# A conditioned feed-forward kernel with its opening rebuilt: who applies bias, deviation and shift, and in which order loads, VectorE's work and row stores stand

## The chip, the cores and the metric

The kernel runs on one core of one Trainium2 chip. A core has TensorE (matmuls, PE in the profile), VectorE (DVE), ScalarE (ACT), GpSimd (POOL) and SyncE (SP, which here only issues DMAs). ScalarE and GpSimd issue DMAs too. The metric is device time in microseconds: the median over runs of the whole execution.

## What is computed

`x` is 32 sequences of 128 tokens by 512 features, `cond` a row of 512 for each sequence, and `mask` marks tokens. With `m` the mask:

```python
emb = silu(t) @ ada_w + ada_b                       # (32, 1536)
shift, scale, gate_msa = split(emb, 3)
norm = layernorm(x) * (1 + scale) + shift
norm = where(m, norm, 0)
fwd = gelu(norm @ ssm_w1 + ssm_b1) @ ssm_w2 + ssm_b2
bwd = gelu(norm @ bwd_w1 + bwd_b1) @ bwd_w2 + bwd_b2
x = x + gate_msa * where(m, fwd + bwd, 0)
...
ff_norm = layernorm(x) * (1 + scale_mlp) + shift_mlp
h = gelu_tanh(ff_norm @ ff_w1 + ff_b1)
return x + gate_mlp * (h @ ff_w2 + ff_b2)
```

All is float32. The flips of the second branch cancel, as each token is worked on alone. The first half matters only for marked tokens, which are the last 0 to 32 of each sequence; the second half is for all 4096.

## The kernel before

The marked tokens are packed into 512 **slots**, four tiles of 128 (`NC`), in the order of their sequences. A matrix `pick` of 128 partitions by 512 slots says which sequence a slot belongs to; its 32 rows stand four times, once for each block of 128 features (`j`). Counting the slots of each sequence gives a column of token numbers, by which GpSimd gathers the tile's rows from `x` (`gather`, L277). Should there be more than 512 marked tokens, a loop at the end deals with the rest; it does nothing in these runs.

The first half works on the slots in two pairs of tiles. For tiles 0 and 1, in the opening:

1. `ada_w`'s shift and scale columns (`ada_a`, four blocks of 128 rows, L150) are loaded first. TensorE multiplies silu(cond), transposed (`sT`), by them into `pm_ss` (L633 to L635). The 32 rows of the four feature blocks lie in the four quarters of the partitions, so four matmuls share the array. The bias gets into the same bank by a matmul of its own, of `quarter` and the four rows `modb` (L294, L576). VectorE copies the sum out into `mod1` (L320).
2. TensorE spreads shift and scale over the slots, by `pick` (`of_slots`, L331; banks `part_s0`).
3. VectorE takes the statistics of a gathered tile (L159 to L162), GpSimd the root of the variance (L164). Then VectorE makes `(x - mean) * scale` in four strips (L356) and `* rstd + shift` in four more (L360).
4. TensorE transposes the tile (L194), ScalarE copies it out (L197), and TensorE multiplies by `w1`: `hidden_of_tile` for the first four blocks of the hidden layer, a tile at a time (L681), then `hidden` for the other four and both tiles together (L205). `w1` holds `ssm_w1` and `bwd_w1` side by side, `w2` both second matrices.

The slots' projections (`project`, L222) are finished by `finish_slots` (L378): gate, add `x`, statistics, and a store of the row with its mean and 1/deviation to `x1_wide` in DRAM. GpSimd gathers from there, over the loaded `x` tiles of the first eight sequences (`raw`, four tiles of two sequences), the rows that the first half changed (`take_first_rows`, L817). VectorE normalises these eight (L847): four are turned by VectorE and DMAs, four by TensorE (L950). All later sequences read `x1_rows`. The second half then runs over four pairs of four sequences each, as block products with sums in the manner of Strassen: `fw1_of.combine` (L403) and `weight_sums` (L741) make the sums of the weights. TensorE's matmuls L1123 and L1310 are this half.

The order on each engine is that of the source, since a manual schedule covers all five (L445). The names `on_zeros` and `keep_clock` are matmuls whose results nothing reads. Loads stand on SP's queue in the source's order; `load_behind_gathers` (L137) lets a GpSimd write to the tile first, so that the load is issued after the gather ahead of it on GpSimd. Each DMA of SP or ScalarE takes the next of eight semaphores, and its issue waits for the DMA that had it before.

Of the kernel before, what the change touches and what calls it, by code (L numbers as in the profile page):

```python
# [9 lines left out]
F32 = mybir.dt.float32  # L10
# [12 lines left out]
def kernel(  # L23
# [88 lines left out]
    nc.sync.dma_start(t_sb, cond)  # L112
# [37 lines left out]
    load_ada(ada_a, ada_w, range(KC), 2 * D)  # L150
# [143 lines left out]
    def modulation_bias(pm):  # L294
        nc.tensor.matmul(
            pm[:, : 2 * P],
            quarter,
            modb[:KC, :2],
            start=True,
            stop=True,  # L300
            skip_group_check=True,
        )

    def modulation_matmuls(pm, ada, lo, hi, blocks, begun=False):
        kinds = ada.rearrange("p k (m d) -> p k m d", d=D)
        for k in blocks:
            for j in range(KC):
                nc.tensor.matmul(
                    pm[ts(j, B), : (hi - lo) * P],
                    sT[:, k, :],  # L310
                    kinds[:, k, lo:hi, ts(j, P)],
                    start=(k == 0 and not begun),
                    stop=True,
                    skip_group_check=True,
                )

    def modulation_rows(pm, mod, lo, hi, bias=None):
        view = pm[:, : (hi - lo) * P].rearrange("p (m c) -> p m c", c=P)
        if bias is None:
            nc.vector.tensor_copy(mod[:, lo:hi], view)  # L320
            return
# [56 lines left out]
    def finish_slots(at, po, gate):  # L378
# [5 lines left out]
        nc.sync.dma_start(x1_wide[ts(at, P), :], t[:, 0])  # L384
        return lambda: nc.sync.dma_start(x1_rows[ts(at, P), :], row)
# [71 lines left out]
    nc.vector.memset(zeros, 0.0)  # L457
    pm_keep_clock = ps_h.tile([P, 512], F32, tag="h", name="pm_keep_clock")
# [73 lines left out]
    nc.gpsimd.tensor_scalar(modb[:KC, 1], modb[:KC, 1], 1.0, None, ALU.add)  # L532
# [43 lines left out]
    quarter = adap.tile([KC, P], F32, name="quarter")  # L576
    nc.scalar.copy(
        quarter.rearrange("p (j b) -> p j b", b=B), ident[:KC, :KC].unsqueeze(2).to_broadcast([KC, KC, B])
    )
# [34 lines left out]
    pick_slots(ts(1, NH))  # L614

# [3 lines left out]
    nc.vector.tensor_scalar(slot_of, slot_of, FAR, None, ALU.add)  # L619

# [16 lines left out]
    modulation_rows(pm, mod1, 0, 2)  # L637

    strips = of_slots(pick, (0, 1), mod1, slice(0, 2), 3 * [(ps_o, "o")] + [(ps_h, "h")], "part_s0")
# [3 lines left out]
    xn = group_of_tiles("s")  # L643
    xn_s = []
    for c in range(2):
        mv, rstd = statistics(xc[c : c + 1], f"s{c}")
        xn_s.append(
            modulated_by_strips(xc[c], strips, c, xn[:, c], mv[:, 0, 0:1], rstd, xn[:, 2 + c])
        )
        if c == 0:  # L650
            for n in range(2):
                nc.tensor.matmul(
                    pm_keep_clock[:, ts(n, 2 * P)], ident, xn[:, 2, ts(n, 2 * P)], start=True, stop=True
                )
            token_i = counted(slots_of_late, slot_col[:, NC // 2 :], NC // 2, "s1", ssm)
            late_slots()
            gather(xc[2], token_i[:, 0:1])
# [32 lines left out]
    transposed_slots(xn_s[0], xT_s[:, :, ts(0, P)], "s0")  # L690
    ptr = ps_t.tile([P, 512], F32, tag="tr", name="ptr_b")
    nc.tensor.transpose(ptr[:, :n_bias], bias_rows, ident[:n_bias, :n_bias])
    nc.tensor.transpose(ptr[:, n_bias : n_bias + B], slot_of, ident[:B, :B])
    nc.scalar.copy(biasT, ptr[:, :n_bias])
    slot_i = const.tile([P, B], I32, name="slot_i")
    nc.vector.tensor_copy(slot_i, ptr[:, n_bias : n_bias + B])
    for f in range(KC):
        hidden_of_tile(f, 0)
    transposed_slots(xn_s[1], xT_s[:, :, ts(1, P)], "s1")
# [90 lines left out]
    for c in range(2):  # L790
        if c == 0:
            own_statistics(raw[0], 2, "x_0")
# [37 lines left out]
    store_rows.append(finish_slots(1, project(1, h1, w2, "s1", seeded=po_s[1]), gs[1]))  # L830
    for i in range(2, 2 * G):
        take_first_rows(i)
# [26 lines left out]
    modulation_rows(pm, mod2, 0, 3, modb)  # L859
    normalised_of_side_0(range(2))  # L860
# [839 lines left out]
```

## Time and profile before

| What | Value |
|---|---|
| median of 3 runs | 452.73 us (452.65 to 452.76) |
| the profiled execution, own time | 453.43 us |
| its span | 451.7 us |
| TensorE busy | 444.0 us |
| VectorE busy | 334.5 us |
| ScalarE busy | 177.9 us |
| GpSimd busy | 158.4 us |
| HBM read, written | 56.71 MB, 13.70 MB |

The span runs from the first to the last instruction that the profiler saw; the execution's own time has some start and end around it. Busy shares are over the whole span, while the change is in its first sixth. For the opening one reads the timeline (start, length, engine, line, what is written from what, how many, and the idle time before them with what ended it). Each float32 matmul stands there as two rows. The DMA rows of the span's first stretch (us, moved until then, summed over all queues):

| until | 4 | 8 | 10 | 12 | 16 | 21.72 | 36.36 | 48.1 |
|---|---|---|---|---|---|---|---|---|
| MB | 0.39 | 2.06 | 2.43 | 3.11 | 4.53 | 6.67 | 12.48 | 16.76 |

Loads and their landing, as far as the trace shows them: the first gather is issued at 6.95 and lands after 3.7 us, the second 8.49 and 6.4; the third column block of `ada_a` 9.59 and 9.1; `ada_f`, the second half's conditioning matrix, has its last block issued at 33.3 and landed after 14.8.

### The profile page before, as it was taken

The page shows a single profiled execution, that of the slowest core. Times are in us where ns is not written, and L with a number is a line of the kernel's source. Part 1 is how long each engine was busy: PE and PEld are TensorE (multiplying, and loading weights), DVE is VectorE, ACT ScalarE, POOL GpSimd, SP SyncE. Part 2 cuts the span into 40 slices and gives each one's busy share as a digit, 9 for nine tenths or more (in the row PEclk, how much of TensorE's full clock was granted, in tenths as well). Part 3 has the DMA queues.
Part 4 walks back from the last instruction along what each step waited for, and adds up shares of the span by engine and source line. Part 5 has one row for each costly group of instructions (what it writes and reads, how often), then busy time and mean ns, then how long its engine had stood idle before and what let it go on. Part 6 is the DMA issues. An engine that isn't in the chain of part 4 may idle for free.

```text
span 451.7 us, 6204 instructions
## 1 busy us (share of the span) xinstructions
PE 444.0 (98%) x2147; PEld 370.2 (82%) x2147; DVE 334.5 (74%) x573; ACT 177.9 (39%) x389; POOL 158.4 (35%) x154
## 2 busy tenths in 40 slices
PE   8999999999999999999999999999999999999995
PEld 3884675688888888888888888888888888888884
DVE  5797788877799759977895689878956885434645
ACT  3123116353651551536526415464265244642000
POOL 4211470089770000897600007977000027560000
PEclk9999999999999999999999999999999999999999
DMA  6999449857327717741396177512971534122022
GB/s 250 372 399 408 177 65 308 284 187 229 129 97 168 108 49 268 235 138 36 105 177 93 46 267 230 141 38 86 189 99 47 176 128 129 35 93 95 0 94 96
DMA packets 85440, 70.84 MB, mean 157 GB/s; under 512 B 63396, under 2 KB 64508, under 8 KB 84382
## 3 DMA queue, kind: packets, MB, share of 16 engines
q1 hardware_dynamic: 64270, 57.76, 42.3%
q0 software_dynamic: 4160, 10.54, 6.9%
q10 hardware_dynamic: 16976, 2.11, 3.9%
q8 instruction: 18, 0.29, 0.3%
q14 instruction: 16, 0.13, 0.1%
HBM read 56.71 MB, written 13.70 MB: 156 GB/s over the span
## 4 chain that ended last, share of the span: by engine, by line
PE 84%; DMA 8%; DVE 3%; issue 2%; POOL 1%; SPq 0%; POOLq 0%
PE a_o L1310 24%; PE a_m L1123 21%; PE e_o L1310 18%; PE e_m L1123 16%; DMA fw<-in_L_cond_ff_w_dram 3%; PE po_s L222 3%; DMA w<-in_L_cond_bwd_w_dram 3%; DMA x_wide<-t_s 2%; DMA x<-x_wide,slot_i 1%; DVE t L403 1%; PE last L1310 1%; PE a_m_alone L1123 1%; POOL x L819 1%; PE ptr L950 0%; PE pl_s L255 0%
## 5 line engine op out<-in xcount | busy, mean ns | idle before, releaser
L1174 POOL TENSOR_TENSOR ha<-p_m,ha 128x512 f32<-128x512 f32 x20 | 25.8, 1292 | 176.0 <-ACT ha L1181 166.1
L1310 PE MATMUL e_o<-fw,ha 128*128 128x256 f32 x256 | 57.9, 379 | 0.0
L944 ACT ACTIVATE xT<-xT,modT 128x128 f32<-128x128 f32 x112 | 44.0, 480 | 28.1 <-DMA xT<-xn 28.1
L1310 PE MATMUL a_o<-t,hb 128*128 128x256 f32 x240 | 54.1, 379 | 0.0
L1310 PEld LDWEIGHTS e_o<-fw,ha 128*128 128x128 f32 x256 | 48.6, 190 | 6.6
L1310 PEld LDWEIGHTS a_o<-t,hb 128*128 128x128 f32 x240 | 45.6, 190 | 6.2
L1085 ACT ACTIVATE hb<-hb,biasT 128x256 f32<-128x256 f32 x64 | 29.0, 500 | 28.3 <-POOL hb L1207 16.1
L1137 ACT COPY p_m<-e_m 128x512 f32<-128x512 f32 x27 | 15.8, 586 | 51.6 <-PE e_m L1123 51.6
L890 POOL DMA_INDIRECT x<-x_rows,slot_i x24 | 27.2, 1135 | 6.2 <-issue 5.4
L1174 POOL TENSOR_TENSOR hb<-p_m,hb 128x512 f32<-128x512 f32 x20 | 29.2, 1460 | 0.3
L1310 PE MATMUL a_o<-fw,ha 128*128 128x256 f32 x128 | 28.9, 379 | 0.0
L1310 PE MATMUL a_o<-t,s 128*128 128x256 f32 x128 | 28.9, 379 | 0.0
L1310 PE MATMUL e_o<-fw,s 128*128 128x256 f32 x128 | 28.9, 379 | 0.0
L222 PE MATMUL po_s<-w,h_s 128*128 128x512 f32 x64 | 28.4, 594 | 0.0
L1181 ACT COPY ha<-e_m 128x512 f32<-128x512 f32 x32 | 18.5, 579 | 24.8 <-PE e_m L1123 24.4
L1310 PEld LDWEIGHTS a_o<-fw,ha 128*128 128x128 f32 x128 | 24.3, 190 | 3.3
L1310 PEld LDWEIGHTS a_o<-t,s 128*128 128x128 f32 x128 | 24.3, 190 | 3.3
L1310 PEld LDWEIGHTS e_o<-fw,s 128*128 128x128 f32 x128 | 24.3, 190 | 3.3
L1148 DVE TENSOR_TENSOR e_m<-a_m,ha 128x512 f32<-128x512 f32 x20 | 14.0, 698 | 17.0 <-POOL ha L1174 7.6
L1085 ACT ACTIVATE ha<-e_m,biasT 128x256 f32<-128x256 f32 x48 | 20.0, 468 | 14.4 <-PE e_m L1123 14.4
L1123 PE MATMUL a_m<-xT,tw 128*128 128x256 f32 x96 | 24.7, 380 | 0.0
L1123 PE MATMUL e_m<-s,fw 128*128 128x256 f32 x92 | 23.7, 380 | 0.0
(234 smaller groups left out, 894.1 us busy)
## 6 DMA issues: line engine op xcount, KB each, us to landing
x<-in_x_dram SPq DMA_DIRECT2D x16, 512.0 KB, 5.9
tw<-t_rows SPq DMA_DIRECT2D x16, 512.0 KB, 4.3
gate<-gate_rows POOLq DMA_DIRECT2D x8, 1024.0 KB, 5.1
out_dram<-x SPq DMA_DIRECT2D x15, 512.0 KB, 4.7
tw<-t_rows SPq DMA_DIRECT2D x16, 384.0 KB, 3.9
xT<-xn SPq DMA_DIRECT2D x80, 64.0 KB, 2.7
ada_f<-in_L_cond_ffada_w_dram SPq DMA_DIRECT2D x4, 768.0 KB, 14.8
ada_a<-in_L_cond_ada_w_dram SPq DMA_DIRECT2D x4, 512.0 KB, 3.6
```

The costliest lines, as they stand in the source:

```text
L222: nc.tensor.matmul(po, h[f][:, ts(i, P)], w[:, f, :], start=(f == 0 and seeded is None), stop=(f == HC - 1), skip_group_check=seeded is no ...
L403: engine.tensor_tensor(out, x, y, ALU.subtract)
L819: nc.gpsimd.indirect_dma_start(out=raw[i // 2][:, i % 2], out_offset=None, in_=x1_wide[:slots], in_offset=bass.IndirectOffsetOnAxis(ap=slo ...
L890: nc.gpsimd.indirect_dma_start(out=xs[i // G][i % G // 2][:, i % 2], out_offset=None, in_=x1_rows, in_offset=bass.IndirectOffsetOnAxis(ap= ...
L944: nc.scalar.activation(out, src, AF.Identity, bias=shift, scale=scale)
L1085: nc.scalar.activation(dst[:, n], src[:, n], AF.Gelu_apprx_tanh, bias=biasT[:, f : f + 1])
L1123: nc.tensor.matmul(bank[:, ts(n, QT)], self.w_block(j, product)[:, ts(n, P)], self.x_block(j, product), start=(product in ("P1", "P5") and ...
L1137: nc.scalar.copy(p5, e)
L1148: nc.vector.tensor_tensor(e, a, p5, add)
L1174: nc.gpsimd.tensor_tensor(self.place(RESULT[j], c), self.p5[j], other, ALU.add)
L1181: nc.scalar.copy(self.place(RESULT[j], c), src)
L1310: nc.tensor.matmul(part, src[:, k, ts(i, P)], w[product][:, k, :], start=(last and k == 0), stop=True, skip_group_check=True,)
```

## The change

- **Bias.** The bias matmul, `quarter` and GpSimd's addition of 1 are gone. `modb` is loaded as rows repeated for 32 sequences, and VectorE adds it as it takes scale and shift out of `pm_ss`, one after the other. The last block of `ada_a` is loaded and multiplied in two halves, scale first. `pm_ss` has a bank of `ps_h`.
- **Deviation and shift.** For tiles 0 and 1 VectorE makes only `(x - mean) * scale`. The transposes become matmuls: of the tile by a diagonal matrix `unit` with 1/deviation on it (ScalarE makes it from the identity), added to a matmul of `shift_of`, the shift in four diagonal blocks, by `pick`. Four plain matmuls and four transposes' worth of matmuls stand where four transposes stood. For tiles 2 and 3 nothing changes here.
- **Scale strips** are made for one tile at a time, the second tile's between the first tile's transposes and its hidden layer.
- **Loads.** `ada_a` is first on SP; `cond` goes to ScalarE's queue, behind the mask. The first four column blocks of `w1` come in two halves, each behind a gather, and the gate columns of `ada_a` after them, behind no gather of their own.
- **Order.** The transposes of the bias rows and of `slot_of` go ahead of the last block of `pm_ss`, and `slot_of` ahead of the late `pick`. The statistics of `raw[0]` go behind the two late tiles, those of `raw[2]` behind the second finish and the gathers of `raw[1]`, those of `raw[3]` behind `mod2`, with the gathers of each tile behind its statistics.
- **Row stores.** The first `x1_wide` store is issued by ScalarE.
- **Filler.** One `on_zeros(256)`, one round of `keep_clock` and the two matmuls on the scaled tile are gone.

The diff, cut to its core:

```diff
-    nc.sync.dma_start(t_sb, cond)
+    nc.scalar.dma_start(t_sb, cond)
...
-    nc.sync.dma_start(modb[:KC, :2], ada_b[: 2 * D].rearrange("(m j c) -> j m c", m=2, c=P))
...
-    load_ada(ada_a, ada_w, range(KC), 2 * D)
+    load_ada(ada_a, ada_w, range(KC - 1), 2 * D)
+    for m in (1, 0):
+        nc.sync.dma_start(ada_a[:, KC - 1, ts(m, D)], ada_w[ts(KC - 1, P), ts(m, D)])
+    for m in (1, 0):
+        load_conditioning_bias(modb[:, m : m + 1], ada_b, (m,))
...
-    nc.gpsimd.tensor_scalar(modb[:KC, 1], modb[:KC, 1], 1.0, None, ALU.add)
+    xn = group_of_tiles("s")
+    shift_of = xn[:, 2].rearrange("p (j c) -> p j c", c=P)
+    unit = [xn[:, 3, ts(c, P)] for c in range(2)]
+    nc.gpsimd.memset(shift_of, 0.0)
...
-        if c:
-            on_zeros(256)
...
-            load_behind_gathers(w1[:, :, :D], ssm_w1)
-    load_behind_gathers(ada_a[:, :, 2 * D :], ada_w[:, 2 * D :])
+            load_behind_gathers(w1[:, :, : D // 2], ssm_w1[:, : D // 2])
+    load_behind_gathers(w1[:, :, D // 2 : D], ssm_w1[:, D // 2 :])
+    load_blocks(ada_a[:, :, 2 * D :], ada_w[:, 2 * D :])
...
-    pm = ps_o.tile([P, 512], F32, tag="o", name="pm_ss")
-    modulation_bias(pm)
-    modulation_matmuls(pm, ada_a, 0, 2, range(KC), begun=True)
+    modulation_matmuls(pm_ss, ada_a, 0, 2, range(KC - 1))
+    ptr = ps_t.tile([P, 512], F32, tag="tr", name="ptr_b")
+    nc.tensor.transpose(ptr[:, :n_bias], bias_rows, ident[:n_bias, :n_bias])
+    nc.tensor.transpose(ptr[:, n_bias : n_bias + B], slot_of, ident[:B, :B])
...
+    for m in (1, 0):
+        modulation_matmuls(pm_ss, ada_a, m, m + 1, (KC - 1,), m)
+    nc.vector.scalar_tensor_tensor(mod1[:, 1], pm_ss[:, ts(1, P)], 1.0, modb[:, 1], ALU.add, ALU.add)
+    nc.vector.tensor_tensor(mod1[:, 0], pm_ss[:, ts(0, P)], modb[:, 0], ALU.add)
+
+    in_four = 3 * [(ps_o, "o")] + [(ps_t, "tr")]
+    scales = of_slots(pick, (0,), mod1, slice(1, 2), in_four, "scale_s0")
     slots_of_late = slots_to_count(pick[:, NH:], NC // 2, "s1", (ps_h, "h"))
...
-    keep_clock(2, 0)
...
+    for j in range(KC):
+        nc.scalar.copy(shift_of[ts(j, B), j], mod1[ts(j, B), 0])
+
+    def with_shifts(c, banks):
...
+        for k in range(KC):
+            nc.tensor.matmul(
+                parts[k],
+                shift_of[:, k],
+                pick[:, ts(c, P)],
+                start=(k % each == 0),
+                stop=False,
+                skip_group_check=True,
+            )
+        return t, parts
+
+    def scaled_slots(c, scales):
         mv, rstd = statistics(xc[c : c + 1], f"s{c}")
...
+        nc.scalar.activation(unit[c], ident, AF.Identity, scale=rstd[:, 0:1])
+        for j in range(KC):
+            nc.vector.scalar_tensor_tensor(
+                xn[:, c, ts(j, P)],
+                xc[c][:, ts(j, P)],
+                mv[:, 0, 0:1],
+                scales[j][:, 0, 0],
+                ALU.subtract,
+                ALU.mult,
+            )
+
+    def in_features(c, t, parts):
+        for k in range(KC):
+            nc.tensor.matmul(
+                parts[k], xn[:, c, ts(k, P)], unit[c], start=False, stop=True, skip_group_check=True
+            )
...
+    keep_clock(1, 0)
+    parts_0 = with_shifts(0, ((ps_t, "tr"), (ps_h, "h")))
+    scaled_slots(0, scales)
+    in_features(0, *parts_0)
+    scales = of_slots(pick, (1,), mod1, slice(1, 2), in_four, "scale_s1")
+    token_i = counted(slots_of_late, slot_col[:, NC // 2 :], NC // 2, "s1", ssm)
+    late_slots()
+    gather(xc[2], token_i[:, 0:1])
+    scaled_slots(1, scales)
...
-    transposed_slots(xn_s[0], xT_s[:, :, ts(0, P)], "s0")
...
     for f in range(KC):
         hidden_of_tile(f, 0)
-    transposed_slots(xn_s[1], xT_s[:, :, ts(1, P)], "s1")
+    in_features(1, *with_shifts(1, ((ps_t, "tr"),)))
...
-    own_statistics(raw[1], 2, "x_1")
+    for n in range(2):
+        own_statistics(raw[n], 2, f"x_{n}")
...
-    own_statistics(raw[2], 2, "x_2")
...
-    store_rows = [finish_slots(0, project(0, h1, w2, "s0", seeded=po_s[0]), gs[0])]
+    store_rows = [finish_slots(0, project(0, h1, w2, "s0", seeded=po_s[0]), gs[0], nc.scalar)]
...
-    own_statistics(raw[3], 2, "x_3")
...
-    for i in range(2, 2 * G):
+    store_rows.append(finish_slots(1, project(1, h1, w2, "s1", seeded=po_s[1]), gs[1], nc.sync))
+    for i in range(2, G):
+        take_first_rows(i)
+    own_statistics(raw[2], 2, "x_2")
+    for i in range(G, G + 2):
         take_first_rows(i)
...
     modulation_rows(pm, mod2, 0, 3, modb)
+    own_statistics(raw[3], 2, "x_3")
+    for i in range(G + 2, 2 * G):
+        take_first_rows(i)
```

More of the change, by code (lines that the diff above doesn't have):

```diff
@@ L292, in late_slots, with modulation_matmuls @@
         xc.extend(both[:, c] for c in range(NC // 2))
[L294 to L304, printed above, removed]
+    def modulation_matmuls(pm, ada, lo, hi, blocks, at=0):
         kinds = ada.rearrange("p k (m d) -> p k m d", d=D)
@@ L308, in modulation_matmuls @@
                 nc.tensor.matmul(
-                    pm[ts(j, B), : (hi - lo) * P],
+                    pm[ts(j, B), at * P : (at + hi - lo) * P],
                     sT[:, k, :],
                     kinds[:, k, lo:hi, ts(j, P)],
-                    start=(k == 0 and not begun),
+                    start=(k == 0),
                     stop=True,
@@ L315, in modulation_matmuls, with modulation_rows @@
                 )
-    def modulation_rows(pm, mod, lo, hi, bias=None):
+    def modulation_rows(pm, mod, lo, hi, bias):
         view = pm[:, : (hi - lo) * P].rearrange("p (m c) -> p m c", c=P)
-        if bias is None:
-            nc.vector.tensor_copy(mod[:, lo:hi], view)
-            return
         other = slice(0, hi - lo, 2)
@@ L376, in gates_of_slots, with finish_slots @@
         return [t[:, n] for n in range(len(tiles))], to_sbuf
-    def finish_slots(at, po, gate):
+    def finish_slots(at, po, gate, queue):
         t = tp.tile([P, 1, D + 2], F32, tag="t", name=f"t_s_{at}")
@@ L383, in finish_slots @@
         own_statistics(t, 1, f"s_{at}_x1")
-        nc.sync.dma_start(x1_wide[ts(at, P), :], t[:, 0])
+        queue.dma_start(x1_wide[ts(at, P), :], t[:, 0])
         return lambda: nc.sync.dma_start(x1_rows[ts(at, P), :], row)
@@ L457 @@
     nc.vector.memset(zeros, 0.0)
+    pm_ss = ps_h.tile([P, 512], F32, tag="h", name="pm_ss")
     pm_keep_clock = ps_h.tile([P, 512], F32, tag="h", name="pm_keep_clock")
@@ L575 @@
     nc.scalar.copy(sT.rearrange("p k b -> p (k b)"), ptr[:, : KC * B])
[L576 to L579, printed above, removed]
     warm = stp.tile([1, 1], F32, tag="warm", name="warm", bufs=1)
@@ L613 @@
     load_blocks(w2[:, :KC], ssm_w2)
-    pick_slots(ts(1, NH))
     slot_of = adap.tile([B, S], F32, name="slot_of")
@@ L619 @@
     nc.vector.tensor_scalar(slot_of, slot_of, FAR, None, ALU.add)
+    pick_slots(ts(1, NH))
     mod1 = const.tile([P, 3, P], F32, name="mod1")
@@ L631, in keep_clock @@
                 )
-    pm = ps_o.tile([P, 512], F32, tag="o", name="pm_ss")
-    modulation_bias(pm)
-    modulation_matmuls(pm, ada_a, 0, 2, range(KC), begun=True)
+    modulation_matmuls(pm_ss, ada_a, 0, 2, range(KC - 1))
+    ptr = ps_t.tile([P, 512], F32, tag="tr", name="ptr_b")
+    nc.tensor.transpose(ptr[:, :n_bias], bias_rows, ident[:n_bias, :n_bias])
+    nc.tensor.transpose(ptr[:, n_bias : n_bias + B], slot_of, ident[:B, :B])
+    nc.scalar.copy(biasT, ptr[:, :n_bias])
+    slot_i = const.tile([P, B], I32, name="slot_i")
@@ L636 @@
+    nc.vector.tensor_copy(slot_i, ptr[:, n_bias : n_bias + B])
+    for m in (1, 0):
[4 more added lines that the diff above has]
+    scales = of_slots(pick, (0,), mod1, slice(1, 2), in_four, "scale_s0")
     slots_of_late = slots_to_count(pick[:, NH:], NC // 2, "s1", (ps_h, "h"))
-    modulation_rows(pm, mod1, 0, 2)
@@ L639 @@
-    strips = of_slots(pick, (0, 1), mod1, slice(0, 2), 3 * [(ps_o, "o")] + [(ps_h, "h")], "part_s0")
-    keep_clock(2, 0)
     xT_s = ssm.tile([P, KC, NH], F32, tag="xT", name="xT_s0", bufs=2)
     xT_t = ssm.tile([P, KC, NH], F32, tag="xT", name="xT_s1", bufs=2)
-    xn = group_of_tiles("s")
-    xn_s = []
-    for c in range(2):
-        mv, rstd = statistics(xc[c : c + 1], f"s{c}")
[L647 to L657, printed above, removed]
+    for j in range(KC):
+        nc.scalar.copy(shift_of[ts(j, B), j], mod1[ts(j, B), 0])
@@ new lines, in with_shifts @@
+    def with_shifts(c, banks):
+        t = []
+        for pool, tag in banks:
+            t.append(pool.tile([P, 512], F32, tag=tag, name=f"ptr_s{c}_{len(t)}"))
+        each = KC // len(t)
+        parts = [t[k // each][:, ts(k % each, P)] for k in range(KC)]
+        for k in range(KC):
[8 more added lines that the diff above has]
+        return t, parts
@@ new lines, in scaled_slots @@
+    def scaled_slots(c, scales):
+        mv, rstd = statistics(xc[c : c + 1], f"s{c}")
+        nc.scalar.activation(unit[c], ident, AF.Identity, scale=rstd[:, 0:1])
[13 more added lines that the diff above has]
+            )
+        for half_no in range(2):
+            k = ts(half_no, KC // 2)
+            src = t[half_no % len(t)].rearrange("p (k s) -> p k s", s=P)
+            nc.scalar.copy(
+                xT_s[:, k, ts(c, P)], src[:, : KC // 2] if len(t) == 2 else src[:, k]
+            )
@@ L688, in hidden_of_tile @@
             )
-    transposed_slots(xn_s[0], xT_s[:, :, ts(0, P)], "s0")
[L691 to L696, printed above, removed]
     for f in range(KC):
         hidden_of_tile(f, 0)
-    transposed_slots(xn_s[1], xT_s[:, :, ts(1, P)], "s1")
+    in_features(1, *with_shifts(1, ((ps_t, "tr"),)))
     pm = ps_o.tile([P, 512], F32, tag="o", name="pm_g")
@@ L790 @@
     for c in range(2):
-        if c == 0:
-            own_statistics(raw[0], 2, "x_0")
         mv, rstd = statistics(xc[2 + c : 3 + c], f"s{2 + c}")
@@ L829 @@
         take_first_rows(i)
-    store_rows.append(finish_slots(1, project(1, h1, w2, "s1", seeded=po_s[1]), gs[1]))
-    for i in range(2, 2 * G):
+    store_rows.append(finish_slots(1, project(1, h1, w2, "s1", seeded=po_s[1]), gs[1], nc.sync))
[3 more added lines that the diff above has]
+    for i in range(G, G + 2):
         take_first_rows(i)
```

## The prediction

> **What bounds the kernel now.** I read the page's first part, then the chain of waits of the first 90 us, then the timeline, engine by engine. The page says what the end is made of:
>
> ```profile
> PE 444.0 (98%) x2147; PEld 370.2 (82%) x2147; DVE 334.5 (74%) x573; ACT 177.9 (39%) x389; POOL 158.4 (35%) x154
> ```
>
> TensorE (PE) works or is kept warm nearly always, so a gain is an earlier arrival of its useful work; nothing after the opening is touched. The chain (start, length, what) shows where its queue last waits for someone else:
>
> ```profile
> 10.01 11.69 DMA w<-in_L_cond_bwd_w_dram
> 21.72 14.63 DMA fw<-in_L_cond_ff_w_dram
> 36.37 1.24 DVE t L403
> ...
> 41.38 0.61 DVE st_x L172
> ...
> 46.39 4.75 DMA x_wide<-t_s
> ...
> 54.37 0.58 POOL t_s L176
> 54.97 2.96 DMA x_wide<-t_s
> ...
> 63.43 3.87 DMA x<-x_wide,slot_i
> 67.30 0.03 issue
> 67.32 0.56 DVE xn L847
> 67.92 0.33 PE ptr L950
> ```
>
> Up to 67.92 us the chain is not TensorE's: the load of `fw1`, VectorE's sums, the store of the first slots' rows, eight gathers by GpSimd, the eighth normalised tile. From there TensorE runs without a break that counts. What TensorE did meanwhile, and how near it came (start, length; in brackets the idle time and its releaser):
>
> ```profile
> 7.63 3.64 PE L308 MATMUL pm_ss<-ada_a,sT 128*32 128x256 f32 x32
> 13.08 1.07 PE L625 MATMUL pm_keep_clock<-ada_a,sT 128*32 128x256 f32 x16
> 16.24 3.81 PE L681 MATMUL ph_s<-xT_s,w 128*128 128x128 f32 x32 [0.27 <-issue]
> 19.88 0.60 PE L194 MATMUL ptr_s<-ident,xn_s 128*128 128x128 f32 x4
> 20.41 1.08 PE L308 MATMUL pm_g<-ada_a,sT 128*32 128x128 f32 x32
> 21.58 3.84 PE L681 MATMUL ph_s<-xT_s,w 128*128 128x128 f32 x32
> 66.31 0.49 PE L950 MATMUL ptr<-ident,xn 128*128 128x128 f32 x3
> 67.92 0.33 PE L950 MATMUL ptr<-ident,xn 128*128 128x128 f32 x1 [1.12 <-DVE xn L847]
> ```
>
> So **two paths meet at 67.92**: TensorE's own work, which could have gone on at 66.80 (67.92 - 1.12), and the side chain. The change shortens both. What it is worth is the later of the two.
>
> **TensorE's path, up to the first hidden matmul (L681, 16.24).** A recorded pair is one float32 matmul, so 32 rows are 16 matmuls.
>
> Removed ahead of `pm_ss`: `on_zeros(256)` between the two slot counts (L462, 5.74 to 6.06) and the bias matmul (L295, 6.65 to 7.63). The weights of `pm_ss` are not late: the DMA rows give 2.06 MB moved by 8.0 us, nearly all of `ada_a`, whose last block was used at 10.2. So `pm_ss` starts 1.3 us sooner, at about 6.3. Three of its four blocks take 3 x 0.854 = 2.56 us (3.64 us for four, less the tail), to 8.9; the two transposes of `ptr_b`, moved here, 0.3; the last block in two halves, 2 x 0.43, to 10.05. `modb` arrives as 64 KB broadcasts instead of 4 KB, on a DMA idle then (55 to 109 GB/s at 8.3 to 8.9 us); I cost it nothing, and 1:1 if it lands after 9.8.
>
> VectorE: the second token column was done at 7.69, now about 7.5; three `slot_of` operations (1.1), the late pick (0.85), `slot_i` (0.18), then scale and shift (0.29 each, the row of L323): mod1 is complete at about 10.4. It was 11.76 after the copy L320. But now the first gathered tile binds: issued at 6.95, landed after 3.7 us, at 10.65. The gather's issue needs nothing that moves. Its statistics: 0.69 + 0.18 + 0.15 with gaps, to 11.75; then only four strip operations instead of eight (1.12 for four): 12.9. GpSimd's root (0.58) and ScalarE's scaled identity (0.3, as the copy L577) end at 12.8 beside them. The four ScalarE copies of the shift (0.25 each, near L575's 0.27) end at 11.5.
>
> TensorE meanwhile: scale strips to 10.65, late count 0.86, `keep_clock(1, 0)` 0.85, to 12.3; four shift matmuls and four deviation matmuls, 0.228 each if the clock is full (3.81 us less tail, over 16): 13.2 and 14.1. ScalarE copies a half in 0.33, and the next scale strips take 0.2: **the first hidden matmul at 14.25** instead of 16.24. Its weights: the first half of `w1` needs some 0.4 MB after 3.11 MB at 12.0, the second follows by 14.5 and is used at 16.1.
>
> **The second tile gives much of it back.** Four transposes took 0.53 us (19.88 to 20.41); four shifts and four deviations are 8 x 0.228 = 1.83. From first to second hidden stretch were 5.34 us (21.58 - 16.24): hidden 3.75, transposes 0.53, `pm_g` and the count 1.06. It becomes 14.25 + 3.75 + 1.83 + 1.02 + 0.25 = 21.1. So **TensorE gains only 0.5 us**. VectorE is done with that tile at 16.2 and hides. The gate columns of `ada_a` landed at 18.7, with 0.13 MB more ahead of them 19.0; `pm_g` wants them at 19.8.
>
> Here a rule speaks against the change. The Trainium skill, "TensorE: Matmul & The Clock Gate", section "What's actually happening": a window of 3.4 us decides, and a busy one lifts the half clock. Row first: `pm_ss` took 634 ns a pass, the same form under `keep_clock` 379; the strips (L342) fall from 548 to 374 between 11.83 and 12.1. The clock rose at 12.0 though TensorE had been busy since 3.26[...]. The page's PEclk shows 9 throughout, so it doesn't show this. By the rule the denser stretch from 6.3 would lift the clock at the boundary before, 12.0 - 3.4 = 8.6: strips at 14.0, TensorE's gain 0.75. By the row it is 12.0 again; I take the row. Against: the change takes out filler (one `on_zeros`, four `keep_clock` matmuls, two on `xn`). If the window to 12.0 is not full enough, 15.4 is next.
>
> **The side chain.** The DMA stream decides up to `fw1`: 6.67 MB by 21.72, 12.48 MB by 36.36, about 396 GB/s. The same bytes stand ahead of `fw1`, and the stream starts at 9.6 in both, for the first `w1` load still waits for the first gather (issue 8.31). The SP queue's issue of `fw1` waits for the landing of `bwd_w1` as before. `fw1` lands at 36.3 again, give or take 0.5, and VectorE's sums end at 41.38. The bound is now: `own_statistics(raw[2])` (41.38 to 43.10, 1.7 us) no longer precedes `finish_slots(0)`, whose projection ends at 41. The store's issue moves from 46.39 to 44.65.
>
> Its landing took 4.75 us behind `ada_f` and the biases on SP's queue, the lighter one at 54.97 took 2.96. From ScalarE's queue: the skill, "DMA: Bandwidth & Descriptors", "Issuing engines are not separate DMA queues", says that all queues share 16 engines and another issuer only saves issue time. By that 4.75: lands 49.4; by the nearest row 2.96: 47.6. I take 48.5, for `ada_f` flows till 48.1 and the rings interleave. Behind this store on ScalarE wait the last seed (0.59) and the late copies at 49.1; ScalarE was idle 6.05 us there. GpSimd follows as before (first gather to last landing: 0.81 + 11.48 + 3.87 after the store lands), plus 0.65 for the root of `raw[3]`, now between gathers: 48.5 + 16.0 = 64.5, and the tile is normalised at 65.1.
>
> VectorE takes the moved statistics back: the second finish starts when TensorE's projection ends, 48.66 - 0.5 = 48.15, and lasts 2.55; statistics 1.7; mod2 0.65; statistics 1.75; two tiles 2.4; sums 2.05; two tiles 2.4; 0.3; sums 2.1; four tiles 2.0: **66.05**. It was 67.88. Its `turn` stores start 0.4 us sooner; ScalarE's scaling ended at 79.85 against a use at 82.7, so they stay hidden.
>
> **Sum.** TensorE could go on at 66.80 - 0.5 = 66.3; VectorE is done at 66.05, gathers at 65.1. The resumption moves from 67.92 to 66.3: **1.6 us**. The profiled execution took 453.43 (span 451.7, 1.7 around it), and becomes 451.8; the median of 452.73 is 0.70 below it, so I forecast **451.1**.
>
> **Rivals.**
> - *More*: the clock rises at 8.6, or the first tile lands sooner on the emptier DMA, and TensorE gains 1.4. Then VectorE's row above also starts 0.9 sooner, gathers end at 65.1, and the gain is 2.5: **450.2**. For it: only half of `w1` now stands ahead of the second gather, and TensorE has no gap from 6.3 on. Against: the first gather's 3.7 us, which nothing here shortens.
> - *Given back*: the first hidden matmul no sooner than 15.3 (late `t_sb` on ScalarE's queue behind the mask delays the counts beyond its 0.6 us slack, late `modb`, a gather later by 1 us). TensorE then loses 0.5; 1.12 - 0.5 = 0.6 us: **452.1**, no change to be told. For it: three things now arrive within half a microsecond of their use.
> - *Slower*: the clock stays half until 18.8, the second boundary after 12.0. Shifts and deviations cold take 3.4 instead of 1.83, the first hidden matmul comes at 16.0, and at half speed does 1.4 us of its work by 18.8; the second stretch starts at 24.2, 2.6 late. With 1.12 of slack that is 1.5: **454.2**. It decides once the loss exceeds 1.12. For it: the clock took until 12.0 with more filler. Against: the window from 8.6 is still filled by `pm_ss`, strips, counts and four keep-clock matmuls.
> - *It doesn't do what it says*: the ScalarE store lands no sooner. At 49.4 the last tile is ready at 66.0, still in time; no loss.
>
> **Numbers.** Forecast 0.42, more 0.30, given back 0.15, slower 0.13. A measurement here tells 0.2% (0.9 us) from nothing: faster than 451.8 holds the first two, 0.72; within 0.15; slower 0.13. The range goes from 449.8 (gain 2.9, the store landing at 47.6 and all else hidden) to 452.9 (the whole of the given-back case); the likeliest case alone is 450.7 to 451.6.
>
> **What would show it.** First hidden matmul near 14.25 and second near 21.1; `pm_ss` from 6.3; strips at the fast rate by 12; first row store issued near 44.7 and landed by 48.5; the last transposes of `raw[3]` near 66.3 with no wait to speak of. Wrong if `pm_ss` waits for `ada_a` or for ScalarE's `sT`, if hidden matmuls run cold, if `fw1` lands after 37.5, or if a wait beyond 70 us eats the shift.

## The result, and the profile after

The changed kernel took 457.73 us (median of 4 runs, 456.18 to 458.13) beside 452.75 us for the kernel before on the same chip: ratio 1.0101, interval 1.0075 to 1.0126, **slower by 5.0 us**. Run once more on another chip it took 456.53 (6 runs, 455.56 to 458.85) beside 452.98: 1.0082, interval 1.0061 to 1.0104. A ratio is estimated from the fast executions of both kernels, so it can differ a little from the quotient of the medians. The two profiled executions have spans of 456.4 and 454.9 us (own times 458.13 and 456.70) against 451.7 (453.43) before. Line numbers are those of each kernel's own profile; the changed file is some 30 lines longer from the opening on (L950 became L981, L222 became L225).

TensorE's total hardly moved; the time is in when its work comes. The page's first part:

```profile
PE 445.2 (98%) x2164; PEld 371.7 (81%) x2164; DVE 332.4 (73%) x566; ACT 180.0 (39%) x394; POOL 158.8 (35%) x154
```

The chain of waits of the first changed execution (start, length, what) shows both ends of the loss:

```profile
1.25 4.68 DMA t_sb<-in_cond_dram
5.93 0.02 issue
5.95 0.64 ACT s_sb L564
6.59 0.04 issue
6.63 0.63 PE ptr_s L568 x4
...
60.01 0.85 POOL x L179
...
64.02 0.73 POOL x L179
...
66.38 3.80 DMA x<-x_wide,slot_i
70.18 0.02 issue
70.21 0.56 DVE xn L875
70.77 0.04 issue
70.81 0.47 PE ptr L981
71.28 3.14 PE po_s L225 x4
74.43 0.44 PE ptr L981 x4
```

At the top, the load of the condition, now on ScalarE's queue, lands at 5.93; before, `s_sb` started at 2.72. Below, the eighth gather is issued at 66.38 (before 63.43), with two roots of GpSimd (`POOL x L179`) between the gathers, and TensorE resumes at 70.81 (before 67.92): 2.9 us. The next group (74.43) comes 4.45 us later than before: `po_s` took 3.14 us instead of 1.72. The third of the three parts is a wait of 0.36 us near 93.6 us. 2.9 + 1.4 + 0.4 = 4.7, the difference of the spans. Why `po_s` is slow shows in the windows of that stretch (window, its length, TensorE's busy time and records, granted clock, DMA share, GB/s):

```profile
68.00:70.00 2.00, 0.77 (x5) 1.00 0.94 113
70.00:71.00 1.00, 0.19 (x1) 0.81 1.18 199
71.00:72.00 1.00, 1.00 (x3) 0.50 1.33 113
72.00:73.00 1.00, 1.00 (x3) 0.50 1.43 146
73.00:74.00 1.00, 1.00 (x2) 0.50 1.06 193
74.00:76.00 2.00, 2.00 (x9) 0.99 1.01 393
```

TensorE was idle for most of 68 to 71, and the granted clock fell to half until 74. The second execution had as little work there (0.96 us in 68 to 71, as here) and kept a clock of 1.00. It lost 2.45 at the resumption (70.37) and 0.36 at the later wait, of 3.2 in all. So the resumption is what both share. Its timeline in that execution, TensorE first, then GpSimd (start, length, engine and line, operands, in brackets the idle time and its releaser):

```profile
15.98 3.93 PE L716 MATMUL ph_s<-xT_s,w 128*128 128x128 f32 x32
22.79 3.84 PE L716 MATMUL ph_s<-xT_s,w 128*128 128x128 f32 x32
67.52 0.38 PE L981 MATMUL ptr<-ident,xn 128*128 128x128 f32 x2
68.55 0.33 PE L981 MATMUL ptr<-ident,xn 128*128 128x128 f32 x1 [0.65 <-DVE xn L875]
70.37 0.33 PE L981 MATMUL ptr<-ident,xn 128*128 128x128 f32 x1 [1.49 <-DVE xn L875]
```

```profile
46.33 0.87 POOL L179 TENSOR_TENSOR t_s<-t_s,half 128x1 f32<-128x1 f32 x1 [8.38 <-issue]
53.47 1.09 POOL L844 DMA_INDIRECT x<-x_wide,slot_i  x1 [6.26 <-DMA x_wide<-t_s]
...
59.27 1.02 POOL L179 TENSOR_TENSOR x<-x,half 128x2 f32<-128x2 f32 x1
...
63.44 0.72 POOL L179 TENSOR_TENSOR x<-x,half 128x2 f32<-128x2 f32 x1
...
65.79 1.12 POOL L844 DMA_INDIRECT x<-x_wide,slot_i  x1 [0.31 <-issue]
```

TensorE could have gone on soon after 68.0; the side chain ends last, and it is late by parts that add up. Before, the root of the first finish began at 45.80 and took 0.56, the first gather came at 51.95, the eighth at 63.43. Now the root begins 0.53 later, takes 0.31 longer, the row store from its end to the first gather takes 6.27 instead of 5.59 (0.68), and from first gather to eighth are 12.32 us instead of 11.48 (0.84). Sum 2.36; the eighth was issued 2.36 later.

The first part, 0.53, hides more. The statistics that were moved away took 1.8 us ahead of this finish, and still it starts later, since all before it is late. The opening of this execution shows why (TensorE's two groups, GpSimd's first gather, VectorE's first use of `fw1`):

```profile
6.07 0.63 PE L568 MATMUL ptr_s<-ident,s_sb 32*128 32x32 f32 x4 [0.83 <-ACT s_sb L564]
6.51 1.20 PE L258 MATMUL pl_s<-rank,pick 32*128 32x128 f32 x4
8.42 1.18 POOL L281 DMA_INDIRECT xc<-in_x_dram,token_i_s  x1 [4.45 <-DVE before_s L264]
38.73 1.23 DVE L393 TENSOR_TENSOR t<-fw 128x1024 f32<-128x1024 f32 x1 [1.55 <-DMA fw<-in_L_cond_ff_w_dram]
```

The same gather before:

```profile
6.95 1.24 POOL L278 DMA_INDIRECT xc<-in_x_dram,token_i_s  x1 [2.85 <-DVE token_i_s L270]
```

The slot counts (`pl_s`, of which the gather's token numbers are made) stand behind `ptr_s` in TensorE's queue, and `ptr_s` waits for the condition. So the gather is issued 1.47 us later, the loads behind it start later, and `fw1` is used 2.36 later (before 36.37). The mask is late too, though it did not change its queue, as `ada_a` now goes ahead of all else. First execution, then before:

```profile
4.15 0.21 DVE L529 CAST mask_f<-mask_u 32x128 f32<-32x128 uint8 x1 [2.54 <-DMA mask_u<-in_mask_BxS_bk_dram]
```

```profile
2.88 0.23 DVE L535 CAST mask_f<-mask_u 32x128 f32<-32x128 uint8 x1 [1.28 <-DMA mask_u<-in_mask_BxS_bk_dram]
```

### The profile page after: what moved, and what is told of

Same layout as the page of the kernel before. It is cut to its first block, busy times and chain, and to the rows that moved or that the text cites. A ratio compares the mean times of both kernels' runs of the same rounds, so it can differ in the third digit from the quotient of the medians.

```text
span 456.4 us, 6244 instructions
## 1 busy us (share of the span) xinstructions
PE 445.2 (98%) x2164; PEld 371.7 (81%) x2164; DVE 332.4 (73%) x566; ACT 180.0 (39%) x394; POOL 158.8 (35%) x154
## 4 chain that ended last, share of the span: by engine, by line
PE 93%; DMA 2%; DVE 2%; POOL 2%; issue 1%; ACT 0%; ACTq 0%; POOLq 0%; DVEq 0%
PE a_o L1341 23%; PE a_m L1154 21%; PE e_o L1341 18%; PE e_m L1154 16%; PE po_s L225 6%; PE ph_s L716 2%; PE ph_s L208 2%; POOL x L844 1%; DMA t_sb<-in_cond_dram 1%; DMA x<-x_wide,slot_i 1%; PE pm_ss L301 1%; PE a_m_alone L1154 1%; PE last L1341 1%; PE ptr_s L649 0%; PE ptr_s L674 0%
## 5 line engine op out<-in xcount | busy, mean ns | idle before, releaser
L225 PE MATMUL po_s<-w,h_s 128*128 128x512 f32 x64 | 29.9, 619 | 0.0
```

Of the source, the lines that this page charges most:

```text
L225: nc.tensor.matmul(po, h[f][:, ts(i, P)], w[:, f, :], start=(f == 0 and seeded is None), stop=(f == HC - 1), skip_group_check=seeded is no ...
```

## The experiments

Three theories stood at the start: 1, the small loads moved behind `ada_a` hold the engines; 2, TensorE's own rebuilt work costs; 3, the new order of VectorE's work and the row store cost. The first four runs split the change. Medians beside the kernel before on the same chip; the ratio with its interval.

**The opening alone** (every hunk but the tail's order, gathers and row store).

> The rebuilt opening with all its loads, but with VectorE's order, the gathers and the row store as they were before. Theory 1: the opening holds the whole loss, so 457 to 459 us. Theory 3, the order and the row store: if statistics moved between finish, gathers and normalisation, and the store from ScalarE, are what is late, the time falls to 454 to 455.5.

456.7 us against 453.15: 1.0076 (1.0059 to 1.0093). **The tail's order alone:**

> The kernel before with VectorE's new order, the split gathers and the first row store from ScalarE alone. Theory 1: no loss here. The store issues near 44.7 instead of 46.39 and, at the 5.4 us that it took in the changed kernel, lands near 50.1 instead of 51.14; the last tile is ready near 66.6 instead of 67.88, and TensorE resumes at 66.8: 451.4 to 452.0 us. Theory 3: slower than 453.5.

454.23: 1.0026 (1.0018 to 1.0035). So both halves lose, 3.6 and 1.1 us, and together about what the whole does. The first theory was right on the first, 0.3 us below its range, and wrong on the second. In the opening's profile, its slowest execution (458.50), TensorE comes to the last transposes without a wait and is itself late; more on this under its clock:

```profile
71.39 0.60 PE L978 MATMUL ptr<-ident,xn 128*128 128x128 f32 x4
```

**Only cond on ScalarE's queue**, in the kernel before:

```diff
-    nc.sync.dma_start(t_sb, cond)
+    nc.scalar.dma_start(t_sb, cond)
```

> The kernel before with that one line alone: cond on ScalarE's queue behind the mask; SP starts with the 4 KB of bias and then ada_a, 0.4 us sooner than before. Theory 1: cond is used after 5 us instead of 2.72, TensorE's counts start near 6.3 instead of 5.04, the first gather near 8.2 instead of 6.95, and the time rises by 1 to 2 us (453.7 to 454.8), because everything behind the gather shifts. Theory 2: within 0.5 us of 452.7.

453.67: 1.0012 (1.0005 to 1.0019), 0.5 us: half of what the first theory had at the least, and the most that the second allowed. In its profile TensorE waited 1.38 us for `s_sb`, the first gather was issued 0.95 later, the second hidden stretch started 1.43 later, but the last transpose at L950 only 0.2 later: the old opening had 1.1 us of slack there. And **cond first on SP's queue again**, in the changed kernel, the same line the other way round:

> The changed kernel with one line put back: cond is loaded first on SP's queue again. Theory 1, the small loads: on ScalarE's queue mask and cond (4 and 64 KB) shared the 16 engines with 2 MB of ada_a that SP issued at 0.81, so mask was used at 4.15 instead of 2.88 and cond at 5.95 instead of 2.72; TensorE's counts wait behind cond's transposes, and gather, loads of w1 and fw1 behind the counts. Then mask is used by about 3.3, cond by 3.0, the first gather issues near 7.2 instead of 8.99, the first hidden matmul comes near 14.8 instead of 16.61, fw1 lands near 37.6 instead of 39.4, and the time falls by 2 to 3.5 us from 457.7, to 454.2 to 455.7. Theory 2, the matmuls: what costs is the rebuilt transposes and the new order; the time stays above 456.5 and TensorE still loses to the kernel before between first and second hidden stretch only.

458.46: 1.0127 (1.0105 to 1.0149), no better. The mask was used at 2.82 again, and `pm_ss` did start at 6.24, but the first hidden matmul came at 18.88, not near 14.8. The wait came back one step on, in TensorE's timeline of this kernel:

```profile
6.24 2.79 PE L301 MATMUL pm_ss<-ada_a,sT 128*32 128x256 f32 x24
11.18 0.25 PE L623 MATMUL ptr_b<-ident,bias_rows 16*128 16x16 f32 x1 [2.15 <-DMA bias_rows<-in_L_cond_ff_b_dram]
11.49 1.08 PE L301 MATMUL pm_ss<-ada_a,sT 128*32 128x128 f32 x16
```

The third of the small `bias_rows` loads was issued at 7.48 on ScalarE's queue and landed past 11. The change had set `ptr_b`, which needs it, ahead of the last block of `pm_ss`, which does not; in TensorE's queue the block waited with it. In the changed kernel the late condition had hidden this.

**Both holds removed** (cond first, and the six lines of `ptr_b` back ahead of the first hidden layer), once with the changed tail and once with the old:

> The changed kernel with cond first on SP's queue again and ptr_b's two transposes, biasT and slot_i back ahead of the first tile's hidden layer. Theory A (TensorE's in-order queue was held by small loads: 2.15 us for bias_rows at ptr_b, after 1.4 us for cond): no wait at ptr_b, first hidden matmul at most 16.9 us in place of 18.88, and at least 1.5 us less than the 458.46 of the kernel with cond alone moved: 456.0 to 457.0. Theory B (TensorE stays at half its clock, since the rebuilt opening gives it less to do): first hidden matmul comes forward by less than 1 us since the cold stretch is as long, time above 457.5. Theory C (the tail's order and ScalarE's row store set the end): 458.0 to 458.8, unchanged, since the side chain ends last.

> The same two repairs in the kernel with only the opening rebuilt (the tail's order, gathers and SP's row store as before). Theory A: with both holds gone the opening is no later than that of before; 452.5 to 454.0 against 453.1 of before. Theory B: 455.5 to 456.5 (456.7 without the repairs). Theory C: like A for this kernel, below 454, and the gap to the kernel with the changed tail is 2 us or more.

456.47 (1.0075, 1.0062 to 1.0088) and 455.01 (1.0047, 1.0030 to 1.0064) beside 452.86. Each taken against the kernel before on its own chip, the first loses 1.7 us less than with cond alone (3.6 for 5.3), the second 1.4 less than the opening with neither (2.15 for 3.55; the intervals just overlap). Against the changed kernel itself (1.0101, and 1.0082 when run again) the first gains 1 us or nothing. Its first hidden matmul stood at 18.73, where theory A had 16.9 at most, and TensorE came to L981 at 70.17 without a wait: its half rate lasted until near 18.8 there, as two rows of one form show.

```profile
14.20 2.08 PE L643 MATMUL ptr_s<-pick,xn_s 128*128 128x128 f32 x8
22.40 1.06 PE L643 MATMUL ptr_s<-pick,xn_s 128*128 128x128 f32 x8
```

So the holds are shown in the traces and in the opening's time; they are not all, and what they are worth in the changed kernel is not clear of noise. The second kernel's profile caught an early clock (about 10.5 us), and shows what the rebuilt opening is worth when all goes well:

```profile
15.14 3.84 PE L710 MATMUL ph_s<-xT_s,w 128*128 128x128 f32 x32
18.82 1.06 PE L643 MATMUL ptr_s<-pick,xn_s 128*128 128x128 f32 x8
19.71 1.06 PE L668 MATMUL ptr_s<-xn_s 128*128 128x128 f32 x8
20.70 1.08 PE L301 MATMUL pm_g<-ada_a,sT 128*32 128x128 f32 x32
21.86 3.84 PE L710 MATMUL ph_s<-xT_s,w 128*128 128x128 f32 x32
```

First hidden matmul 1.1 us sooner than before (16.24), second 0.3 later (21.58), since shifts and deviations of the second tile fill 18.82 to 20.70. In this execution the rebuilt arithmetic gives back more than it gains.

**TensorE's clock.** The first kernel has the opening rebuilt, both repairs, and the filler put back (`on_zeros(512, 512)` ahead of `pm_ss`, `on_zeros(256)` between the gathers, `keep_clock(2, 0)`); the second is the kernel before less the filler that the change removes; the third the changed kernel with filler in its waits and every load left.

> The kernel with only the opening rebuilt, both repairs, and TensorE's filler as before: two 128x512 zeros matmuls ahead of the modulation's, the 256-wide one between the two gathers, keep_clock twice in place of once. Theory B: the clock rises at 12 to 13 us, first hidden matmul up to 2 us earlier than without filler and 1 to 2 us less time. Theory A: the filler only adds its own 1 to 2 us of cold matmuls, time the same or up to 1 us more. Theory C: no change from the kernel without filler (within 0.4 us).

> The kernel before less the filler that the change also takes away: the 256-wide zeros matmul between the two gathers, one of the two rounds of keep_clock, the four 128x256 matmuls behind the first tile (about 2.5 us of TensorE's time at half clock); its modulation's bias matmul stays. Clock theory: in part of the executions the clock rises after 16 us in place of 12, and the time is 0.5 to 2 us more than before, with a spread of 2 us or more. If filler is only cost: first hidden matmul 0.5 us or more earlier, time 452.3 to 453.0.

> The changed kernel (457.73 us) with filler alone: two 128x512 zeros matmuls in the wait for the mask and two in that for cond, the 256-wide one between the gathers, keep_clock twice. Every load stays where it is. Clock theory: the clock rises by 14 us, 456.0 to 457.2. Loads theory: 457.3 to 458.5, since the first gather and fw1 stay late and the side chain with them.

The first: 453.95 (11 runs; 1.0021, 1.0009 to 1.0034), 1.1 less than without filler; the two intervals just overlap. The second: 453.67 (21 runs; 1.0023, 1.0011 to 1.0036) in two clusters, sixteen of 452.05 to 454.15 and five of 455.52 to 456.49. Its profiled execution is of the first: span 450.5, less than before's 451.7, second hidden stretch at 21.11. That the clock rises late in the second cluster is likely but not shown, as none of its executions was profiled. Nor is it shown that this filler costs anything when the clock rises in time: the first cluster's median, 453.4, is no lower than the 452.98 of before. And filler does not keep such executions away: the kernel with the tail's order and both stores on SP's queue, further below, has all of it, and four of its 15 executions stand apart at 455.59 to 456.02. None of the kernel before is above 454.23. The third: 457.45 (1.0107, 1.0087 to 1.0127), no gain, though the clock rose before 12 us: there the loads decide, and `fw1` was used at 38.80 again (before 36.37). **The changed kernel again** belongs here:

> The changed kernel once more: 457.2 to 458.2. In its first profile the clock rose at 12.8 us; three of five kernels with the same opening rose at 18 to 20. If the rise varies between executions of one program: it may rise late here, first hidden matmul after 19 us, TensorE itself late at 70 us in place of the side chain, at about the same time. If it is fixed: 16.6 and 66.5 us again.

456.53 us. The rise does vary between executions of one program: 10.6 us here and 12.8 in the first profile. Two kernels with this very opening rose late, at about 20.0 (the opening alone) and 19.6 (the next run), so the changed kernel can be expected to at times, though its two profiles did not catch it. A late rise doesn't need less filler either: the kernel before rose at 12.0 in its profile, and four kernels below that keep its opening and change only the tail rose at about 13 to 17, with the first hidden matmul at 16.60 to 18.57 instead of 16.24. And a late rise changes which path ends last. In all four profiles of the rebuilt opening in which it came past 17 us (the opening alone, cond first, both holds removed with the changed tail, the next run), TensorE reached the last transposes at 70.2 to 71.4 us without a wait: there it was late itself, not only the side chain. One more kernel put eight identity matmuls ahead of each of the last two transposes at L981, to see whether the half clock of 71 to 74 us is usual:

> The changed kernel (457.73 us) with eight 128x128 matmuls of the identity ahead of each of the last two transposes of L981's first group, in the 1.0 and 1.6 us in which TensorE waits there. If the half clock of 71 to 74 us is a usual part of the loss: no clock under 0.95 after 66 us and 456.0 to 457.0. If that was one execution's chance: 457.4 to 458.2. Where the filler itself stands in the way (over 0.15 us each), above 458.2.

459.48 (1.0137, 1.0109 to 1.0164). It tells little: the clock rose only near 19.6 us there, TensorE came to L981 at 71.06 with no wait to fill, and the filler took 1.8 us each time. The second profile of the changed kernel answers instead: the half clock after 70 us was that of one execution of two.

**The DMA stream.** The repaired opening with `w1`'s first half in one load of 2 KB rows, and the gate's weights behind the second gather, as before:

> The kernel with the opening rebuilt, cond first, ptr_b late and filler back (453.95 us), now with w1's first half in one load of 2 KB rows behind the first gather and the gate's weights behind the second, as before. If the 1 KB rows slow the stream: fw1 lands 0.5 to 1 us earlier, 453.0 to 453.5 against 452.9 of before. If they don't (the stream is late because it starts later, or the loss is elsewhere): 453.7 to 454.2, fw1's landing within 0.3 us.

454.6 is the median of six executions, of which one took 1211.67 us for a reason that is not known; the ratio (1.0037, 1.0024 to 1.0051) leaves it out, and the other five have a median of 454.08. VectorE's first use of `fw1` moved from 37.07 to 36.43, where it was before the change, as the first reading had it; the time did not follow, since both executions resume within 0.15 us of before. So `fw1` is not what is left. Whether the 1 KB rows had made it late is not shown: the run also moved the gate's weights, and two executions of the changed kernel differ by as much (39.40 and 38.73).

**The tail's order**, in the kernel before, with both stores on SP's queue:

> The kernel before with the tail's order changed (statistics of raw[2] and raw[3] later, gathers split) but both row stores on SP's queue. Theory C1 (the store from ScalarE's queue lands later and costs what the order gains): first store lands in 4.5 to 4.9 us, time 452.0 to 452.8, below before. Theory C2 (the order itself costs: statistics between the gathers hold the last norms): 454.0 to 454.6, as with ScalarE's queue (454.23).

454.17 (1.0034, 1.0022 to 1.0045), as with ScalarE's queue: the second reading. VectorE and GpSimd in this kernel:

```profile
42.76 0.69 DVE L381 TENSOR_TENSOR t_s<-po_s,gs 128x512 f32<-128x512 f32 x1 [1.02 <-PE po_s L222]
```

```profile
45.46 0.86 POOL L176 TENSOR_TENSOR t_s<-t_s,half 128x1 f32<-128x1 f32 x1 [6.94 <-DVE t_s L175]
52.11 1.08 POOL L816 DMA_INDIRECT x<-x_wide,slot_i  x1 [5.79 <-DMA x_wide<-t_s]
...
57.82 0.90 POOL L176 TENSOR_TENSOR x<-x,half 128x2 f32<-128x2 f32 x1
...
61.84 0.75 POOL L176 TENSOR_TENSOR x<-x,half 128x2 f32<-128x2 f32 x1
...
64.22 1.49 POOL L816 DMA_INDIRECT x<-x_wide,slot_i  x1 [0.30 <-issue]
```

The statistics of `raw[2]` no longer stand ahead of finish 0 (1.8 us), but finish 0 then waits for its projection, 1.02 us, and starts 0.34 sooner than before:

```profile
43.10 0.69 DVE L381 TENSOR_TENSOR t_s<-po_s,gs 128x512 f32<-128x512 f32 x1
```

Part of that wait is the clock's: TensorE was 0.87 late from the first hidden matmul on (17.11). The root after it takes 0.86 instead of 0.56, with VectorE's sums L741 beside it now; it does so in all eleven profiles with a changed tail, and in none of the seven with the old. So the store leaves no sooner. And the roots of `raw[2]` and `raw[3]`, which had run before the gathers, stand between them: 12.11 us from first to eighth instead of 11.48, and the last operand lands at 68.7 instead of 67.3. The test is to leave the order and take the roots out of the way:

```diff
     store_weight_sums(3)
+    own_statistics(raw[2], 2, "x_2")
...
     for i in range(2, G):
         take_first_rows(i)
-    own_statistics(raw[2], 2, "x_2")
+    own_statistics(raw[3], 2, "x_3")
...
-    own_statistics(raw[3], 2, "x_3")
```

> The kernel before with the tail's order changed, stores on SP's queue (454.17 us so), but the statistics of raw[2] taken after the weight sums of block 3, where VectorE waits 2.18 us for po_s, and those of raw[3] after finish 1, their root on GpSimd ahead of gather 4, which waited 1.03 us for the second store in the trace of before. Theory R (the two roots of 0.75 to 0.90 us between gathers 3 and 6 put the last gather at 64.22 in place of 63.43, and that is the order's loss): last gather issued at 63.5 or before, TensorE's last transpose of its group at 68.0 or before, time 452.3 to 453.0. Theory Q (SP's or GpSimd's indirect transfers themselves take longer in the new order): 453.8 to 454.4, last gather after 64.

453.27 (1.0008, 1.0000 to 1.0016), 0.9 less, or 1.0 against before on each chip; eighth gather at 63.07, last transpose at 67.57. Then finish 1, and with it its root, moved ahead of gathers 0 and 1:

> As the run before, and finish 1 with its root ahead of gathers 0 and 1 on GpSimd (there the root stood at 54.4 behind two gathers though VectorE had its input at 51.8). Theory R: the first gather 0.6 us later, the second store 2 us earlier, so that gather 4 no longer waits; last gather at 62.8 to 63.2, time 451.6 to 452.5, less than before. If the row stores' landing doesn't decide: 452.8 to 453.5, since the first gather's 0.6 us is all that counts.

**452.25 us** (13 runs; 0.9982, 0.9973 to 0.9991), the one kernel here that is faster than before. Its profile fell on its slowest execution (own time 454.37), with a late clock:

```profile
18.57 3.81 PE L681 MATMUL ph_s<-xT_s,w 128*128 128x128 f32 x32 [0.27 <-issue]
```

Yet the eight gathers then follow each other in 10.0 us (54.55 to 64.57). TensorE comes to its last transposes without a wait, at 68.64, in part because it was 2.3 us late itself. Last, **everything mended**, the rebuilt arithmetic with this tail:

> The rebuilt opening with cond first, ptr_b late, filler back and w1 in one load, the tail with the roots apart, the second store ahead of the gathers and both stores on SP's queue. If the rebuilt arithmetic has a gain of its own: below the 452.25 us of the old opening with the same tail, 451.2 to 452.0. If its eight shift and eight deviation matmuls of the second tile give it all back: 452.3 to 453.5.

454.46 (1.0036, 1.0023 to 1.0049), 2.2 more than the old opening with the same tail, and above both readings. So the rebuilt opening has no gain of its own here. In its profile the resumption is 0.7 us sooner than before, and this is lost later:

```profile
88.37 1.13 PE L1154 MATMUL e_m<-s,fw 128*128 128x256 f32 x4 [0.36 <-DVE e_m L1179]
```

This wait is in all seven profiles of kernels that have both the rebuilt opening and a changed tail, and in none of the others. Another 0.8 us went after 90 us, most of it in gaps of 0.1 us between 177 and 187 us for which the profile names no releaser; the opening alone and the opening with filler lose time there too (1.4 and 0.7 us). Why is open, and so is a part of what the rebuilt opening still costs when its holds are gone.

## Why the prediction was wrong

It said 451.1 us, with 452.9 as the upper end; the kernel needs some 457. No rival had this size: "slower" said 454.2. The step that failed first is the gather's issue, second below; the terms in their order:

- *`pm_ss` at 6.3.* It started at 8.21. With cond first it was 6.24, so the sum was right and the premise failed: that the condition had 0.6 us of slack and ScalarE's queue was good enough. It came 2.7 to 3.2 us late. The "given back" rival named this load, and then bounded it at 1 us without a row for a 64 KB load beside 2 MB on the other queue.
- *"The gather's issue needs nothing that moves."* This step failed. It put at nothing the wait of `ptr_s` for the moved condition, with `pl_s` behind it, and that of the counts for the mask. The gather was issued at 8.99 and 8.42 instead of 6.95, all later loads behind it; `fw1`, said to land at 36.3, was used at 39.40 and 38.73. The text itself put the limit at 37.5. That the whole loss follows from this is not shown: with the holds removed the opening still lost 2.15 of its 3.55 us.
- *`ptr_b`, 0.3 us.* Its length was right. That it could wait for `bias_rows`, with `pm_ss`'s last block behind it, was not asked: 2.15 us once the other hold was gone.
- *The second tile gives back 1.83.* It took 1.88. The changed kernel's first hidden matmul came at 16.61 and 15.98, not 14.25, its second stretch at 23.33 and 22.79, not 21.1. With the holds removed they were 15.14 and 21.86 at best, so TensorE's path loses 0.3 there instead of gaining 0.5. Where the clock rose at 12.1, as before (the opening with filler), they were 16.24 and 22.96: 1.4 lost.
- *The clock rises at 12.0 by the row.* The row was one execution. The rule of the Trainium skill ("TensorE: Matmul & The Clock Gate", "What's actually happening") that a busy window lifts the clock gave no usable time: with one and the same old opening, TensorE at work from 3.3 us, it rose at 12.0 to about 17 in five profiles. When it rises cannot be read from one trace. The "slower" rival had this mechanism; in the two profiles of the changed kernel the clock rose early, so there it is not the main term.
- *The store issued at 44.65, 1.74 sooner.* It was 47.9 and 47.2. Without the opening's delay it was no sooner than before: the projection that "ends at 41" ended at 41.8 in the kernel before itself and at 42.2 to 42.7 in three of the kernels with that order and the old opening, whose clock rose later, and the root was 0.3 longer.
- *Landing 3.85 us.* 5.5 in the first profile (issue 47.91, gather 54.17 with 0.8 us between landing and gather, as before), more than both ends of the range taken. On the order alone, ScalarE's queue against SP's: first gather 0.27 later, no difference in time. As the Trainium skill has it ("DMA: Bandwidth & Descriptors", "Issuing engines are not separate DMA queues"), another issuer brought nothing.
- *GpSimd +0.65 for one root.* Two roots stood between the gathers, and with them first to eighth gather took 0.36 to 0.84 us more, about what was put down for one. That `raw[2]`'s root moves too was left out, though the sum for VectorE counted its statistics.
- *48.5 + 16.0 = 64.5.* The terms give 16.8: last landing at 65.3, tile at 65.9. The forecast stays, as TensorE's 66.3 is later; but "lands no sooner" would then have ended at 66.8, a loss of 0.5 and not none. Against 65.9 the second execution came 4.4 late: 2.6 at the store's issue, 1.6 from there to the first gather (6.27 instead of 4.66), 0.2 among the gathers.
- *Resumption at 66.3.* 70.81 and 70.37.

The two paths were read rightly, and so was where they meet. In the late gather, `ptr_b` and the roots what failed is the same: a moved item was costed by what it does, not by what stands behind it in the queue that it enters. In the store's landing and the clock, one row of one execution was taken for what the next would do.

## What to carry to other kernels

A tiny load or root is cheap only where nothing in order waits behind it: before moving one, list what follows it on its engine, and whose start that decides. A hold removed shows the next one (cond, then `bias_rows`), so undo them together before judging. When TensorE's half rate ends differed by 2 us between two executions of one program: judge filler, and whatever else changes the opening, by the spread of many executions, not by one profile.

## What the runs showed of the hardware

- A 64 KB load on ScalarE's queue issued at 1.25 us, beside 2 MB issued from 0.81 on SP's, landed after 4.68 and 4.11 us; issued first on SP's queue, before the large loads, it was there by 2.7.
- TensorE's half rate lasted until anything from 10.1 to 20.0 us in programs that differ by a few matmuls. Two executions of one program rose at 10.6 and 12.8, and five programs with the same opening at 12.0 to about 17.
- After 3 us with 0.96 us of work, TensorE's granted clock fell to 0.50 for 3 us in one execution and stayed at 1.00 in another. In the opening, where matmuls also ran at half rate, the record of the granted clock shows no such value.
- GpSimd's root of one column at the first finish took 0.56 us in all seven profiles with the old tail, and 0.86 to 0.88 in all eleven with the changed one, where VectorE's sums of two operands run beside it. That the sums are the reason is likely; no run sets them apart.
